# Row 0 copied and not rotated, biases of q and k as rows, zero columns left out, a sums step moved to the denominators, first sums in a fixed order

## Chip, cores, metric

One core of one Trainium2 chip. The metric is the time of one launch on the device in microseconds (us); where several runs of a kernel exist, their median. Every run quoted here is in the fast state: none took over 1.5% longer than the fastest of its kernel. TensorE is called PE in the profile, VectorE DVE, ScalarE ACT, GpSimd POOL, SyncE SP.

## The reference, cut

Two residual layers on eight images of 256 channels, 96 x 96, in f32.

```python
def gn(v, G=32, eps=1e-5): ...                 # group norm over 8 channels x H x W, no scale or shift
def layer0(x):                                 # after group norm
    q, k, v = [fft2(pconv(x, w, b)) for w, b in ((w1, b1), (w2, b2), (w3, b3))]   # 1x1 convolutions
    # 8 heads of 32 channels; q and k normalised over all positions
    attn = einsum("bhcn,bhdn->bhcd", q, k) * temperature       # complex
    attn = complex(softmax(real(attn)), softmax(imag(attn)))
    return pconv(abs(ifft2(einsum("bhcd,bhdn->bhcn", attn, v))), w_out)
def layer1(x):                                 # after group norm; linear attention, d = 32
    q, k = softplus(Wq x + bq), softplus(Wk x + bk)
    v = Wv x + bv
    norm = 1 / einsum("bnd,bd->bn", q, sum_n(k) + 1e-6)
    return einsum("bnd,bde,bn->ben", q, einsum("bdn,ben->bde", k, v), norm)
x = x + layer0(gn(x))
x = x + layer1(gn(x))                          # x: (8, 256, 96, 96) f32
```

The kernel does not compute an FFT. It takes even and odd parts of each image (a pixel and its mirror), their products over channels ("sums") for layer 0's attention, a "rotation" of each image row, and builds from these the absolute value of layer 0. Layer 1 follows image by image.

## The kernel before

Work of two images is woven on TensorE: a stage is a generator, and at each `yield` a step of another generator is put into TensorE's stream. While image b goes through its stages, the steps of the sums of image b+1 fill the gaps. A stage that yields more takes steps that would otherwise stand at the end of the output stage. (The name `own` is a scratch tile of layer 1, `xr` a transposed row, `y` a rotated row, `eo` the even and odd parts.)

```python
# the sums of one image: a generator; each yield ends one "sums step" = 4 transposes + 8 product passes on TensorE
def pair_sums(b):
    ...
    ahead = [even_odd(b, us.pop(0))]           # sums and differences of a row and its mirror, VectorE or GpSimd
    for u in range(NT - 1, -2, -1):            # u = 0: the rows that are loaded last
        ...
        for i in range(0, cols, P):
            ...
            nc.tensor.transpose(pt[...], eo[:, c, k, i:i + np_], ident)          # eoT
            ...
            products(*pending, first, False)                                    # acc
            if b and u < NT and i:
                stats_chunk(st0, b, 2 * (NT - 1 - u) + i // P - 1)
            yield
    if not b:
        for c in range(NC):
            stats_chunk(st0, b, c)

# in the attention stage: the biases of q and k are added by matmuls against the identity
for c in range(2):
    for m in range(KC):
        nc.tensor.matmul(pb[32 * m:32 * m + 1, c * P:(c + 1) * P], lhsT=b12col[:, KC * c + m:KC * c + m + 1],
                         rhs=ident, start=False, stop=(c == 1), skip_group_check=True)
yield 1
...
# in the rotation of two image rows: transpose, then multiply by the rotation of that row
for r in range(2):
    for k in range(KC):
        if h is not None:
            o = x_col(h + r)
            nc.tensor.transpose(pt[0:W, ...], x_of(b)[:, k, o:o + W], ident)     # xr
        if turned is not None:
            nc.tensor.matmul(pu[:, o:o + W + 1], lhsT=gt[0:W, r, ...], rhs=tm[:, g % TR + r, :], ...)   # y
...
# end of layer 1: denominators, attention map
nc.vector.reciprocal(rec, pd[:, 0:CH])
...
yield 1                                        # one sums step of the next image is put here
# output stage
for s in range(NS):                            # NS = 6 groups of 4 chunks
    for m in range(KC):
        ...                                    # output matmuls, additions to x
        yield 1
    if b + 1 < B and s in (1, NS - 1):
        load_x(b + 1, NT // 4 - 2 - s // 2 // 2)          # the last rows of the next image
    ...                                        # four output transfers of 384 KB

def weave(stage, other):                       # other's steps are put in where the stage yields
    due = 0
    for n in stage:
        due += n
        while due >= 1:
            next(other, None)
            due -= 1

sums = pair_sums(0)
next(sums); tables(); finish(sums)
turns = rotate(0)
for b in range(B):
    weave(attention(b), turns); finish(turns)
    sums = pair_sums(b + 1) if b + 1 < B else iter(())
    weave(images(b), sums)
    weave(layer1(b), sums)
    weave(output(b, *l1.pop(b)), sums)
    if b + 1 < B:
        turns = rotate(b + 1)
        finish(sums)                           # what steps are left come here
```

## Time and profile before

| | before |
|---|---|
| time, median of 4 runs (range) | 2778.5 us (2775.7 to 2780.7) |
| span of the profiled run | 2776.2 us |
| TensorE busy | 2731.4 us, 98% |
| mean granted clock of TensorE | 0.992 |
| TensorE's first instruction | 9.16 us |
| first transposed row of the rotation | 76.97 us |
| period of an image | 341.3 us |

The lines are in the prediction below. For this document the trace is also cut into stages, by the start of TensorE's first instruction of each kind: first transposed row (xr), first sum over rows of the rotated image (zs), first projection of layer 1 (kq), denominators (den), next image's first xr. Such a stage has a length that repeats to 0.02 us from image to image unless TensorE waits in it, so a change of 0.1 us per image can be read from one trace, where the times of whole runs scatter by 2 to 5 us. These stage lengths are read from the timeline and subtracted; the text gives them as plain numbers. The granted clock is the share of its full clock that TensorE got.

### The profile page before, as it was taken

The numbers are of one execution on the slowest core, as the hardware profiler recorded it, in microseconds if no ns is written. First come the engines' busy times: TensorE is split into PE (matmuls) and PEld (weight loads), VectorE is DVE, ScalarE is ACT, GpSimd is POOL, SyncE is SP. The second block draws the span as 40 slices with busy tenths as digits, with TensorE's granted clock in tenths as the row PEclk, the third lists the DMA queues.
The fourth block names the chain that finished last, engine by engine and source line by source line (L and its number), as shares of the span: only waits on it lengthen the run. The fifth ranks groups of instructions, "written<-read, shape, count | busy, mean of one in ns | idle before, by whom it ended". The sixth has DMA issues, their size and how long they took to land.

```text
span 2776.2 us, 47920 instructions
## 1 busy us (share of the span) xinstructions
PE 2731.4 (98%) x18460; PEld 1982.1 (71%) x18460; DVE 1950.3 (70%) x4088; ACT 1374.4 (50%) x2114; POOL 835.8 (30%) x914
## 2 busy tenths in 40 slices
PE   8999999999999999999999999999999999999988
PEld 8965679657795677956679566885678856788556
DVE  6578765876658766587675876758766687666766
ACT  3455634556345563355634546445554455544553
POOL 5033340343403424035140350413513134131311
PEclk9999999999999999999999999999999999999997
DMA  5120151201512015120151201521015210241003
GB/s 168 36 67 12 47 183 43 66 10 49 177 43 72 6 47 181 43 69 6 53 177 45 63 6 53 181 53 52 6 53 184 56 46 7 76 164 27 1 7 137
DMA packets 197810, 192.52 MB, mean 69 GB/s; under 512 B 89360, under 2 KB 197584, under 8 KB 197584
## 3 DMA queue, kind: packets, MB, share of 16 engines
q1 hardware_dynamic: 130336, 164.34, 18.6%
q10 hardware_dynamic: 67248, 25.12, 3.6%
q8 instruction: 147, 2.41, 0.4%
q14 instruction: 79, 0.65, 0.1%
HBM read 113.85 MB, written 75.57 MB: 68 GB/s over the span
## 4 chain that ended last, share of the span: by engine, by line
PE 94%; DVE 3%; ACT 2%; issue 0%; DMA 0%; POOL 0%; POOLq 0%; ACTq 0%; DVEq 0%
PE z L615 20%; PE po L627 18%; PE acc L325 13%; PE y L549 10%; PE xr L546 6%; PE eoT L344 5%; PE xT L773 5%; PE kq L712 5%; PE o L857 4%; PE kx L749 3%; PE cw L423 1%; DVE rec L819 1%; PE kT L764 1%; DVE arena L554 1%; PE mz L510 1%; PE cw L434 1%
## 5 line engine op out<-in xcount | busy, mean ns | idle before, releaser
L615 PE MATMUL z<-arena,mz 128*128 128x384 f32 (+2 forms) x2400 | 595.0, 476 | 0.0
L627 PE MATMUL po<-e,wo 128*128 128x384 f32 x1536 | 529.7, 486 | 0.2 <-ACT e L662 0.2
L661 POOL TENSOR_TENSOR e<-e 128x768 f32<-128x768 f32 x192 | 348.5, 1816 | 553.5 <-ACT e L660 553.5
L615 PEld LDWEIGHTS z<-arena,mz 128*128 128x128 f32 (+1 forms) x2400 | 325.6, 163 | 241.4 <-issue 42.4
L549 PE MATMUL y<-tm,xT 96*128 96x97 f32 x3072 | 477.6, 261 | 1.7 <-ACT sd_a L283 0.5
L549 PEld LDWEIGHTS y<-tm,xT 96*128 96x128 f32 x3072 | 462.6, 192 | 12.9 <-ACT xT L557 5.1
L325 PE MATMUL acc<-xT 128*128 128x256 f32 (+2 forms) x2368 | 440.2, 328 | 3.5 <-ACT xT L347 3.5
L627 PEld LDWEIGHTS po<-e,wo 128*128 128x128 f32 x1536 | 289.5, 190 | 197.7 <-DVE arena L629 1.2
L656 DVE TENSOR_TENSOR e<-z,xT 128x768 f32<-128x768 f32 x384 | 366.1, 953 | 88.2 <-PE z L615 88.2
L259 DVE BATCH_NORM_STATS2 st<-arena 128x6 f32<-128x384 f32 x768 | 406.3, 552 | 14.6 <-DMA arena<-in_x_dram 4.1
L546 PE MATMUL xr<-ident,arena 128*96 128x128 f32 x1536 | 413.6, 275 | 0.0
L325 PEld LDWEIGHTS acc<-xT 128*128 128x128 f32 (+1 forms) x2368 | 380.0, 191 | 37.7 <-ACT xT L347 5.2
L557 ACT COPY xT<-xr 96x512 f32<-96x512 f32 x384 | 222.2, 583 | 287.6 <-PE xr L546 286.1
L660 ACT ACTIVATE e<-e 128x1536 f32<-128x1536 f32 x192 | 284.5, 1482 | 92.6 <-DVE e L656 91.4
L662 ACT ACTIVATE e<-e 128x768 f32<-128x768 f32 x192 | 161.9, 843 | 334.4 <-POOL e L661 333.2
L311 POOL TENSOR_TENSOR eo<-arena 128x760 f32<-128x760 f32 x136 | 247.2, 1818 | 141.9 <-issue 133.3
L629 DVE TENSOR_TENSOR arena<-arena,po 128x384 f32<-128x384 f32 x384 | 211.2, 552 | 94.8 <-PE po L627 71.8
L347 ACT ACTIVATE xT<-eoT 128x512 f32<-128x512 f32 x280 | 166.8, 598 | 189.8 <-PE eoT L344 187.9
L532 POOL COPY tm<-csn 96x6 f32<-96x6 f32 x128 | 24.7, 193 | 752.0 <-PE y L549 549.7
L546 PEld LDWEIGHTS xr<-ident,arena 128*96 128x96 f32 x1536 | 230.1, 150 | 8.9 <-issue 5.6
L554 DVE COPY arena<-y 128x384 f32<-128x384 f32 x384 | 210.3, 548 | 0.8
L553 DVE COPY ys<-y 128x4 f32<-128x4 f32 x384 | 62.5, 163 | 207.2 <-PE y L549 205.1
(200 smaller groups left out, 3073.8 us busy)
## 6 DMA issues: line engine op xcount, KB each, us to landing
arena<-in_x_dram SPq DMA_DIRECT2D x184, 384.0 KB
out_dram<-arena SPq DMA_DIRECT2D x184, 384.0 KB
tm<-rt ACTq DMA_DIRECT2D x112, 216.0 KB
tm<-rt SPq DMA_DIRECT2D x16, 216.0 KB
arena<-in_x_dram SPq DMA_DIRECT2D x8, 288.0 KB
out_dram<-arena SPq DMA_DIRECT2D x8, 288.0 KB
wl<-in_w1t_dram SPq DMA_DIRECT2D x8, 256.0 KB
wl<-in_w2t_dram SPq DMA_DIRECT2D x8, 256.0 KB
```

Source lines behind the costliest of these rows:

```text
L259: nc.vector.bn_stats(out=st[:, k, c, :], in_=x_of(b)[:, k, c * CH:(c + 1) * CH])
L311: op(d[:, :, lo:hi, 1:W], x_t[:, :, ra:ra + n, 1:W], x_t[:, :, back, W - 1:0:-1])
L325: mm = nc.tensor.matmul(acc[c][:, m * C:m * C + (KC - m) * P], lhsT=t[0:np_, c, m * P:(m + 1) * P], rhs=t[0:np_, c, m * P:C], start=(first ...
L546: nc.tensor.transpose(pt[0:W, r * C + k * P:r * C + (k + 1) * P], x_of(b)[:, k, o:o + W], ident)
L549: nc.tensor.matmul(pu[:, o:o + W + 1], lhsT=gt[0:W, r, k * P:(k + 1) * P], rhs=tm[:, g % TR + r, :], start=True, stop=True)
L554: nc.vector.tensor_copy(y[:, :, :, g:g + 2], src[:, :, W - 1::-1, :])
L557: nc.scalar.copy(xt[0:W, :, 0:C], pt[0:W, :].rearrange("p (r n) -> p r n", r=2))
L615: mm = nc.tensor.matmul(out[:, o:o + n * W], lhsT=columns(mz, k, c, j), rhs=y[:, k, h * W:(h + n) * W], start=(k == 0 and o == 0), stop=(k ...
L627: nc.tensor.matmul(po[:, 0:CH], lhsT=wo[:, k, m * P:(m + 1) * P], rhs=e[:, k, :], start=(k == 0), stop=(k == KC - 1))
L656: nc.vector.tensor_add(e[:, 2 * c:2 * c + 2, :].rearrange("p t (q h) -> p t q h", h=H), pz[:, 0:CH].rearrange("p (q h) -> p q h", h=H).uns ...
L660: nc.scalar.activation(e, e, AF.Square)
L661: nc.gpsimd.tensor_add(e[:, 0:2, :], e[:, 0:2, :], e[:, 2:4, :])
```

## The change

Its intent: fewer instructions on TensorE, which is the bound (parts 1 to 3), one wait of TensorE covered by work (part 4), and an earlier start (part 5).

1. Row 0 of each image is turned by nothing, so it is copied by GpSimd; its two transposes and two matmuls go.
2. The biases of q and k lie as rows and are added by VectorE, in place of four matmuls per image.
3. 24 zero columns of a small matrix are set by a memset and not by matmuls.
4. One more sums step stands between the denominators and the broadcast of their reciprocal; the last loads are asked for ahead of the sums step that follows the output matmuls.
5. VectorE's instructions of the first image's sums are kept in program order, ahead of the table copies.

```diff
@@ -126,7 +126,10 @@
     def ps_tile(name):
         return psum.tile([P, 512], F32, tag="ps", name=name)
 
+    loaded = set()
+
     def load_x(b, t):
+        loaded.add((b, t))
         for c in (2 * (NT - 1 - t), 2 * (NT - 1 - t) + 1):
             for h, n in chunk_rows(c):
                 nc.sync.dma_start(out=x_of(b)[:, :, x_col(h):x_col(h) + n * W], in_=x_v[b, :, :, h * W:(h + n) * W])
@@ -189,14 +192,16 @@
     wkq0 = const.tile([P, KC, 2, D], F32, name="wkq0")
     for c, v in enumerate((wkt, wqt)):
         nc.scalar.dma_start(out=wkq0[:, :, c, :], in_=v.rearrange("(k p) o -> p k o", p=P))
-    b12col = const.tile([P, 4], F32, name="b12col")
+    b12 = const.tile([P, 2, P], F32, name="b12")
     b3col = const.tile([P, KC], F32, name="b3col")
     bkq4 = const.tile([P, 2], F32, name="bkq4")
     tcol = const.tile([P, KC], F32, name="tcol")
 
     def load_small():
+        nc.gpsimd.memset(b12[0:64], 0.0)
         for c, v in enumerate((b1, b2)):
-            nc.sync.dma_start(out=b12col[:, KC * c:KC * c + KC], in_=v.rearrange("(k p) -> p k", p=P))
+            for m in range(KC):
+                nc.sync.dma_start(out=b12[32 * m:32 * m + 1, c, :], in_=v[m * P:(m + 1) * P].unsqueeze(0))
         nc.sync.dma_start(out=b3col, in_=b3.rearrange("(k p) -> p k", p=P))
         temp_f = temp.rearrange("h a b -> h (a b)")
         for h in range(C // HEAD):
@@ -290,6 +295,7 @@
 
     def even_odd(b, u):
 
+        assert (b, u % NT) in loaded
         nr = PR if u < NT else 1
         t = ring_tile(f"eo_{b}_{u}").rearrange("p (c k n) -> p c k n", c=2, k=KC)
         x_t = image(x_of(b))
@@ -350,12 +356,9 @@
                     products(*pending, first, False)
                     first = False
                 pending = (t, np_)
-                if b and u < NT and i:
+                if u < NT and i:
                     stats_chunk(st0, b, 2 * (NT - 1 - u) + i // P - 1)
                 yield
-        if not b:
-            for c in range(NC):
-                stats_chunk(st0, b, c)
         s0[b] = st0, acc, products, pending
 
     y0 = {}
@@ -388,16 +391,13 @@
             for m in range(KC):
                 nc.tensor.matmul(pb[32 * m:32 * m + 2, 0:2 * P], lhsT=dmm[:, k, :],
                                  rhs=w12[:, k, :].rearrange("p (c n) -> p c n", c=2)[:, :, m * P:(m + 1) * P],
-                                 start=(k == 0), stop=False, skip_group_check=True)
-        for c in range(2):
-            for m in range(KC):
-                nc.tensor.matmul(pb[32 * m:32 * m + 1, c * P:(c + 1) * P], lhsT=b12col[:, KC * c + m:KC * c + m + 1],
-                                 rhs=ident, start=False, stop=(c == 1), skip_group_check=True)
+                                 start=(k == 0), stop=(k == KC - 1), skip_group_check=True)
         yield 1
 
         qkm = [scr[1][32 * m:32 * m + 2, 0:6 * P].rearrange("p (i c n) -> p i c n", i=3, c=2) for m in range(KC)]
         for m in range(KC):
-            nc.scalar.copy(qkm[m][:, 0], pb[32 * m:32 * m + 2, 0:2 * P].rearrange("p (c n) -> p c n", c=2))
+            nc.vector.tensor_add(qkm[m][:, 0], b12[32 * m:32 * m + 2],
+                                 pb[32 * m:32 * m + 2, 0:2 * P].rearrange("p (c n) -> p c n", c=2))
             nc.vector.tensor_scalar_mul(qkm[m][:, 1], qkm[m][:, 0], hw2[32 * m:32 * m + 2])
             nc.vector.tensor_mul(qkm[m][:, 2], qkm[m][:, 0], qkm[m][:, 1])
         pt = ps_tile(f"covT_{b}")
@@ -504,12 +504,13 @@
 
         MZ = (NZ + 3) * NH
         mz = one.tile([P, KC, MZ], F32, tag="wbig", name=f"mz_{b}")
+        nc.gpsimd.memset(mz[:, :, NZ * NH:MZ], 0.0)
         for k in range(KC):
             pm = ps_tile(f"mz_{b}_{k}")
             for m in range(KC):
-                nc.tensor.matmul(pm[:, 0:MZ], lhsT=w3n[:, m, k * P:(k + 1) * P],
-                                 rhs=at[:, m].rearrange("p n h -> p (n h)"), start=(m == 0), stop=(m == KC - 1))
-            nc.vector.tensor_scalar_mul(mz[:, k, :], pm[:, 0:MZ], rstd[:, k:k + 1])
+                nc.tensor.matmul(pm[:, 0:NZ * NH], lhsT=w3n[:, m, k * P:(k + 1) * P],
+                                 rhs=at[:, m, 0:NZ].rearrange("p n h -> p (n h)"), start=(m == 0), stop=(m == KC - 1))
+            nc.vector.tensor_scalar_mul(mz[:, k, 0:NZ * NH], pm[:, 0:NZ * NH], rstd[:, k:k + 1])
             yield 1
 
         m0[b] = mz, nmean, beta
@@ -525,6 +526,9 @@
 
         y = image(y_of(b))
         ys = one.tile([P, KC, H + 1], F32, tag="ys", name=f"ys_{b}")
+        o = x_col(0)
+        nc.gpsimd.tensor_copy(y[:, :, :, 0], x_of(b)[:, :, o:o + W])
+        nc.gpsimd.memset(ys[:, :, 0:1], 0.0)
 
         def load_r(h):
             tm = three.tile([P, TR * (W + 1)], F32, tag="tm", name=f"tm_{b}_{h}")[0:W].rearrange("p (r w) -> p r w", r=TR)
@@ -541,20 +545,22 @@
                 pu = ps_tile(f"y_{b}_{g}")
             for r in range(2):
                 for k in range(KC):
-                    if h is not None:
+                    if h is not None and h + r:
                         o = x_col(h + r)
                         nc.tensor.transpose(pt[0:W, r * C + k * P:r * C + (k + 1) * P], x_of(b)[:, k, o:o + W], ident)
-                    if turned is not None:
+                    if turned is not None and g + r:
                         o = (r * KC + k) * (W + 1)
                         nc.tensor.matmul(pu[:, o:o + W + 1], lhsT=gt[0:W, r, k * P:(k + 1) * P], rhs=tm[:, g % TR + r, :],
                                          start=True, stop=True)
             if turned is not None:
                 src = pu[:, 0:2 * KC * (W + 1)].rearrange("p (r k w) -> p k w r", r=2, k=KC)
-                nc.vector.tensor_copy(ys[:, :, g:g + 2], src[:, :, W, :])
-                nc.vector.tensor_copy(y[:, :, :, g:g + 2], src[:, :, W - 1::-1, :])
+                r = 0 if g else 1
+                nc.vector.tensor_copy(ys[:, :, g + r:g + 2], src[:, :, W, r:2])
+                nc.vector.tensor_copy(y[:, :, :, g + r:g + 2], src[:, :, W - 1::-1, r:2])
             if h is not None:
                 xt = xt_slot()
-                nc.scalar.copy(xt[0:W, :, 0:C], pt[0:W, :].rearrange("p (r n) -> p r n", r=2))
+                r = 0 if h else 1
+                nc.scalar.copy(xt[0:W, r:2, 0:C], pt[0:W, r * C:2 * C].rearrange("p (r n) -> p r n", n=C))
                 return xt
 
         tms = [load_r(g) for g in range(0, 3 * TR, TR)]
@@ -822,7 +828,7 @@
             nc.tensor.matmul(pa[:, 0:C], lhsT=kxT[:, k, :], rhs=wvs[:, k, :], start=(k == 0), stop=(k == KC - 1))
         am = own[:, 3 * C + 4:4 * C + 4]
         nc.vector.scalar_tensor_tensor(am, in0=bvs, scalar=ksum, in1=pa[:, 0:C], op0=ALU.mult, op1=ALU.add)
-        yield 1
+        yield 2
 
         l1[b] = x, kq, rec, am
 
@@ -868,9 +874,9 @@
                     if s + 1 >= 4:
                         pds.append(select(s + 1, acc_tile(f"rec_{b}_{s + 1}")))
                     normalize(s + 1, pds[s + 1])
+                if b + 1 < B and m and s in (1, NS - 1):
+                    load_x(b + 1, NT // 4 - 2 - s // 2 // 2)
                 yield 1
-            if b + 1 < B and s in (1, NS - 1):
-                load_x(b + 1, NT // 4 - 2 - s // 2 // 2)
             for j in range(NB):
                 for h, n_ in chunk_rows(NB * s + j):
                     nc.sync.dma_start(out=out_v[b, :, :, h * W:(h + n_) * W], in_=x[:, :, x_col(h):x_col(h) + n_ * W])
@@ -889,9 +895,11 @@
             pass
 
     sums = pair_sums(0)
-    next(sums)
-    tables()
-    finish(sums)
+    with tc.manual_schedule(engines={mybir.EngineType.DVE}):
+        for _ in range(NT):
+            next(sums)
+        tables()
+        finish(sums)
     turns = rotate(0)
     for b in range(B):
         with tc.manual_schedule(engines={mybir.EngineType.PE}):
```

## The prediction

> **What bounds the kernel now.** I read the profile page first, then the waits of the matrix engine (PE), then timelines of four places. From the page:
>
> ```profile
> PE 2731.4 (98%) x18460; PEld 1982.1 (71%) x18460; DVE 1950.3 (70%) x4088; ACT 1374.4 (50%) x2114; POOL 835.8 (30%) x914
> PE 94%; DVE 3%; ACT 2%; issue 0%; DMA 0%; POOL 0%; POOLq 0%; ACTq 0%; DVEq 0%
> ```
>
> PE is busy for 98% of the span and carries 94% of the chain that ends last. Every PE instruction taken out therefore shortens the run by its place in the stream, and work moved between DVE, ACT and POOL costs nothing unless PE comes to wait for it. The waits of PE (columns: waiter, releaser, total us, times, longest) show how little waiting is left:
>
> ```profile
> PE eoT L344 <- DVE eo L311: 9.4, 2, 9.2
> PE rec L833 <- DVE rec L819: 5.2, 8, 1.6
> PE eoT L344 <- POOL eo L312: 1.3, 7, 0.2
> ```
>
> The first is the start of the kernel, the second the wait for the reciprocal of the denominators, once per image. The timeline says what the start waits for (start, duration, idle before and its releaser):
>
> ```profile
> 6.01 0.39 POOL L312 TENSOR_TENSOR eo<-arena 128x8 f32<-128x8 f32 x2 [2.50 <-DMA arena<-in_x_dram]
> 7.28 0.18 DVE L234 COPY gsel<-arena 128x16 f32<-128x16 f32 x1 [2.14 <-DMA arena<-in_gmat_dram]
> 8.08 1.80 DVE L311 TENSOR_TENSOR eo<-arena 128x760 f32<-128x760 f32 x2
> 9.16 0.66 PE L344 MATMUL eoT<-ident,eo 128*128 128x128 f32 x2 [9.16 <-DVE eo L311]
> ```
>
> The rows for the first even/odd sums are in by 6.01 (POOL uses them), but DVE stands behind copies that wait for a small table until 7.28 and starts the sums at 8.08; PE follows 1.08 us later. From then on PE runs one sums step (4 transposes, 8 product passes) each 1.75 us, without a gap, until 77 us. An image then takes 341.2 us (matching PE lines at 77 and 418).
>
> **What the Trainium skill says.** "TensorE: Matmul & The Clock Gate", section "LDWEIGHTS (loading the stationary operand)": a weight load takes its columns over 1.2 GHz, 80 ns for 96 and 107 ns for 128. The trace agrees where it matters: in the rotation one transpose (96 weight columns) and the two passes of one matmul (128 each) make 80 + 107 + 107 = 294 ns, and the pattern repeats every 307 ns. The same page, "Back-to-back issue gap": about one column per cycle at 2.4 GHz. The trace's f32 passes need two cycles per column (eight passes of 384 columns in 2.58 us, 322 ns each), and a matmul of the program is two passes. "SBUF — State Buffer", section "SBUF: two separate sides": DVE and GpSimd lock a shared port for a whole instruction, so one blocks the other when both read two SBUF operands. The trace agrees: the first long POOL sum, at 8.88, takes 2.65 us instead of 1.8 while DVE is in its own.
>
> **Part 1, row 0 not rotated.** The timeline of PE at the start of image 2's attention:
>
> ```profile
> 418.44 1.04 PE L546 MATMUL xr<-ident,arena 128*96 128x128 f32 x8
> 423.29 0.28 PE L546 MATMUL xr<-ident,arena 128*96 128x128 f32 x1
> 423.40 0.36 PE L549 MATMUL y<-tm,xT 96*128 96x97 f32 x2
> 423.69 1.03 PE L389 MATMUL qkm<-wl,dmm 128*2 128x256 f32 x8
> 424.55 0.61 PE L394 MATMUL qkm<-ident,b12col 128*1 128x128 f32 x8
> 425.09 0.31 PE L546 MATMUL xr<-ident,arena 128*96 128x128 f32 x1
> ```
>
> Eight transposes occupy 418.44 to 419.32, so one is 0.11 us; a transpose with its two y passes is 0.307, so a y is 0.20. Two transposes and two y go: 2 x 0.11 + 2 x 0.20 = 0.62 us per image, **-5.0 us** for eight. The copy instead is one POOL instruction of 192 elements per partition, by scale with POOL's 1.0 us for 384 (two operands) about half a microsecond. In the built order it stands in the prologue among the sums, and for later images behind the last sums, where POOL idles 14 us (its tm copy at 423.83). It must wait for the output transfers of the image before, as the first y write of DVE did. I count nothing for it.
>
> **Part 2, biases.** L394 goes: 424.55 to 425.09 is 0.54 us per image, **-4.3 us**. The ACT copies (0.75 us for the two) become two DVE additions of 2x256, about 0.4 us each by the neighbouring DVE products (L402, 0.40). Their result is first used by matmuls at 438.8, thirteen microseconds later: nothing.
>
> **Part 3, zero columns.** Four matmuls of two passes lose 24 columns each: 8 x 24 x 2 / 2.4 = 160 ns per image, **-1.3 us**. A pass still has 264 columns (220 ns), above its 107 ns weight load.
>
> **Part 4, a sums step at the denominators.** Before, in image 1:
>
> ```profile
> 364.62 1.13 PE L822 MATMUL am<-wvs,own 128*128 128x256 f32 x4
> 365.58 0.60 PE L344 MATMUL eoT<-ident,eo 128*128 128x128 f32 x4
> 366.02 0.82 PE L325 MATMUL acc<-xT 128*128 128x256 f32 x4
> 367.35 0.93 PE L833 MATMUL rec<-rec,sel 32*128 32x384 f32 x8 [0.52 <-DVE rec L819]
> ```
>
> One sums step more before L833 covers the 0.52 us. It exists for seven images (the eighth has no next image): total 5.2 less the 1.6 of the last, **-3.6 us**. The step is not free: it comes from the end of the output stage, where seven steps followed the last output matmuls. The fourth last of all steps needs the image's last loaded rows (eo of u=0), and the load waits for those output matmuls:
>
> ```profile
> 401.95 1.22 PE L857 MATMUL o<-arena,own 32*128 32x384 f32 x8
> 407.83 1.42 DVE L311 TENSOR_TENSOR eo<-arena 128x570 f32<-128x570 f32 x2 [1.68 <-DMA arena<-in_x_dram]
> 410.15 0.60 PE L344 MATMUL eoT<-ident,eo 128*128 128x128 f32 x4
> ```
>
> From the start of the last output group, DVE could begin after 5.88 us and finished its second sum after 7.30; PE came at 8.20. Now PE comes one step (1.75) earlier, at 6.45, and reaches the two transposes that need the second sum at 6.67. In the seven images the DVE start lies at 5.88, 6.97, 5.22, 6.11, 5.4, 5.55 and 5.34; adding about 1.5 for the second sum and its wrapped column on POOL, less 6.67 (6.95 in the last, where PE came 0.28 later): waits of 0.7, 1.8, 0.05, 0.95, 0.25, 0.4, 0, together **+4.1 us**. The move thus gives back what it takes. Moving the issue of the load ahead of the sums step does not help: its transfer still waits for the same matmuls.
>
> **Part 5, first sums in fixed order.** DVE now does the first sums before any table copy, so it starts at about 6.0 instead of 8.08: PE starts about 2.1 us earlier. One table matmul also leaves PE's start (10.61 to 11.34 before) for a place where it costs next to nothing. The next sums come from POOL: their rows are in at 8.88, then two instructions of 1.8 and two of 0.2, 12.9 at best, 13.7 as before with the port lock; PE wants them at about 13.5. I take **-2.4 us**. Later DVE has to keep up with PE: in the built order it will stand at the table matmul until PE's step 12, near 29 us, and still has about 4 us before PE needs its next sums (13.5 + 15 x 1.75 = 39.8 against about 35.5).
>
> Sum: -5.0 - 4.3 - 1.3 - 3.6 + 4.1 - 2.4 = -12.5, so 2778.4 - 12.5 = **2765.9 us**, some 0.45% faster.
>
> **Rivals.** (A) The load of the last rows is no worse than before or lands earlier: then all of part 4 counts and the sum is -16.6, 2762. For it: three of the seven landings leave almost no wait. Against it: image 2 already waits a little at this place (the 1.3 us of waits above, seven times in all), so there is no reserve. (B) The load lands later, because output and input share the engines and the moved step shifts them: 2 us per image gives +14 instead of +4.1, about 2776, no gain. For it: landings vary by 1.75 us now. Against it: the load stands in the same order behind the same transfers. (C) The fixed DVE order makes PE wait in the prologue, for example at the table matmul, by a few microseconds: 2768 to 2772. Against it: the 4 us of reserve worked out above. (D) The longer DVE chain in the attention stage, or POOL behind the row copy, stalls PE: each us per image would cost 8. The slack of 13 us and POOL's 14 us of idleness speak against it.
>
> **Range and chances.** A and the best prologue (-0.5) give about 2761; B in part, or C, gives 2772. With 3 us of scatter between the runs of before I take 2760 to 2773. Leaving 2% (55 us) either way needs something none of these holds: within 2% 0.98.
>
> **What would show it right or wrong.** PE's first transpose near 7.1 us and the first rotation near 74.6. No L394, and 0.54 us less there. PE busy falls by about 11. The wait of rec for DVE falls to the last image's, about 1.6 us. A wait of eoT, by DVE or POOL eo, of about 4 us in seven pieces appears near the end of each output stage. The period of an image falls from 341.2 to about 340.0 (-0.62 - 0.54 - 0.16 - 0.52 + 0.6 = -1.24). I am wrong if the new eoT waits are absent or several times larger, if PE's start doesn't move, or if PE waits at the denominators as before.

## The result

| | before | after |
|---|---|---|
| time, median of 4 runs (range), us | 2778.5 (2775.7 to 2780.7) | 2763.6 (2762.5 to 2765.0) |
| ratio after/before | | 0.9947, 95% interval 0.993 to 0.9964 |
| predicted | | 2766 (2760 to 2773) |

Ratios are the mean time of one kernel's fast runs over that of the other's of the same rounds, so not quite the ratio of the medians quoted. A control of five further rounds in a later call gave 2765.1 us (2762.6 to 2767.8) against 2776.2, ratio 0.996 (0.9948 to 0.9973). The record calls two kernels different from 2% on, so by its measure the time is the same; but both intervals leave out 1, so a small gain is there.

From the page of the changed kernel (busy time with share and instructions; then the shares of the chain that ended last by engine):

```profile
PE 2719.5 (99%) x18348; PEld 1972.5 (71%) x18348; DVE 1958.4 (71%) x4104; ACT 1366.5 (49%) x2098; POOL 841.5 (30%) x939
PE 94%; DVE 3%; ACT 2%; DMA 1%; issue 1%; POOL 0%; SPq 0%; POOLq 0%; DVEq 0%; ACTq 0%
```

TensorE's busy time fell by 11.9 us; it is still the bound. DMA rose from 0% to 1% of the chain. The waits of TensorE (us in all, times, longest) say why:

```profile
PE eoT L350 <- POOL eo L318: 10.4, 15, 7.3
...
PE rec L839 <- DVE rec L825: 1.6, 1, 1.6
```

The wait for the reciprocal is down from eight to the one of the last image. The wait of the transposes (eoT) for POOL's part of the even and odd sums has 15 pieces. Two are the kernel's start (7.3 and 0.2). Seven, 1.3 us in all, stand 129.6 us after the start of zs in each image in which sums run, and were there before the change. Six, 1.6 us in all, are new: they stand at the end of the output stage of three images. (The view lists only waits above 0.15 us.) The start itself, from the timeline (start, duration, what; in brackets the idle time before it and its releaser):

```profile
6.19 1.82 DVE L317 TENSOR_TENSOR eo<-arena 128x760 f32<-128x760 f32 x2 [3.54 <-DMA arena<-in_x_dram]
7.29 0.67 PE L350 MATMUL eoT<-ident,eo 128*128 128x128 f32 x2 [7.29 <-POOL eo L318]
...
30.12 0.15 DVE L246 COPY arena<-pcs 96x2 f32<-96x2 f32 x1 [2.07 <-PE pcs L244]
```

DVE goes to the sums when their rows are in, and TensorE starts at 7.29 and not at 9.16. The third line is the place where DVE stands for a table matmul; TensorE did not wait there.

The stages of the two profiled runs:

| from, to | before | after | difference in the run |
|---|---|---|---|
| start, first xr | 76.97 | 75.05 | -1.9 |
| xr, zs (attention and rotation), each of images 2 to 8 | 74.90 | 73.69 | 8 x -1.21 = -9.6 |
| zs, kq, all eight | 1161.6 | 1161.5 | -0.1 |
| kq, den, images 1 to 7 | 65.06 to 65.08 | 65.05 to 65.08 | -0.1 |
| kq, den, last image | 57.78 | 55.27 | -2.5 |
| den, next xr, sum of seven | 387.22 | 385.61 | -1.6 |
| last den, TensorE's end | 30.04 | 30.08 | 0.0 |

Together -15.8 us between these two traces (-15.5 between the spans, as the last transfers end 7.6 us after TensorE before and 7.9 after). Two lines need explaining: 2.5 us in the last image, where the change did nothing, and den to xr, where a wait of 0.52 us went from each of seven images and yet the sum fell by only 1.6. In that stage TensorE has at the denominators

```profile
363.93 1.47 PE L331 MATMUL acc<-xT 128*128 128x256 f32 x8
365.33 0.93 PE L839 MATMUL rec<-rec,sel 32*128 32x384 f32 x8
```

without a wait before the broadcast (0.52 in the lines of before). And at the end of the output stage, first the queue of SP (which asks for the transfers), then VectorE, then TensorE:

```profile
399.48 2.69 SPq L135 DMA_DIRECT2D arena<-in_x_dram  x3
402.26 4.24 SPq L882 DMA_DIRECT2D out_dram<-arena  x5
```

```profile
404.49 0.62 DVE L317 TENSOR_TENSOR eo<-arena 128x190 f32<-128x190 f32 x2 [1.86 <-DMA arena<-in_x_dram]
405.79 1.42 DVE L317 TENSOR_TENSOR eo<-arena 128x570 f32<-128x570 f32 x2 [0.67 <-DMA arena<-in_x_dram]
```

```profile
406.69 0.42 PE L350 MATMUL eoT<-ident,eo 128*128 128x128 f32 x2 [0.16 <-POOL eo L318]
407.36 0.42 PE L350 MATMUL eoT<-ident,eo 128*128 128x128 f32 x2 [0.26 <-POOL eo L318]
```

Follow the chain upwards: TensorE waits for POOL's small part of eo (L318), which comes with VectorE's (L317), which waits for the rows of the last load (asked for from 399.48). This is the wait that the prediction set against the covered one. The brackets show 0.16 + 0.26 = 0.42 us of idle time, but that stage (the first of the seven) takes 55.47 us where one without a wait takes 54.65: the wait costs 0.82. The starts of the timeline tell it: these transposes begin 1.64 us after the products ahead of them, the ones before began 1.31 after theirs, and the second pair starts 0.67 after the first, where without a wait it starts 0.22 after. In two later images the wait cost 0.9 and 1.1 us (0.50 and 0.71 shown), in one 0.2, in three nothing. So the cost is no multiple of the idle time shown: where both pairs show a wait, it is 0.4 us more.

### The profile page after: what moved, and what is told of

Its sections match the earlier page's. It is cut to its first block, busy times and chain, and to the rows that moved or that the text cites. A ratio compares the mean times of both kernels' runs of the same rounds, so it can differ in the third digit from the quotient of the medians.

```text
span 2760.7 us, 47785 instructions
## 1 busy us (share of the span) xinstructions
PE 2719.5 (99%) x18348; PEld 1972.5 (71%) x18348; DVE 1958.4 (71%) x4104; ACT 1366.5 (49%) x2098; POOL 841.5 (30%) x939
## 4 chain that ended last, share of the span: by engine, by line
PE 94%; DVE 3%; ACT 2%; DMA 1%; issue 1%; POOL 0%; SPq 0%; POOLq 0%; DVEq 0%; ACTq 0%
PE z L621 21%; PE po L633 18%; PE acc L331 13%; PE y L553 10%; PE xr L550 6%; PE eoT L350 5%; PE xT L779 5%; PE kq L718 5%; PE o L863 4%; PE kx L755 3%; DMA arena<-in_x_dram 1%; PE cw L423 1%; PE kT L770 1%; DVE arena L559 1%; PE mz L511 1%
## 5 line engine op out<-in xcount | busy, mean ns | idle before, releaser
L553 PEld LDWEIGHTS y<-tm,xT 96*128 96x128 f32 x3040 | 457.8, 192 | 12.5 <-issue 4.9
L563 ACT COPY xT<-xr 96x512 f32<-96x512 f32 (+1 forms) x384 | 220.2, 578 | 293.8 <-PE xr L550 289.4
L317 POOL TENSOR_TENSOR eo<-arena 128x760 f32<-128x760 f32 x136 | 246.1, 1809 | 253.7 <-issue 130.1
L559 DVE COPY arena<-y 128x384 f32<-128x384 f32 (+1 forms) x384 | 209.7, 547 | 1.2 <-issue 0.5
L558 DVE COPY ys<-y 128x4 f32<-128x4 f32 (+1 forms) x384 | 62.4, 162 | 199.3 <-PE y L553 195.9
L350 PE MATMUL eoT<-ident,eo 128*128 128x128 f32 (+1 forms) x1184 | 188.1, 280 | 10.4 <-POOL eo L318 10.4
```

What stands on the lines that cost most here:

```text
L317: op(d[:, :, lo:hi, 1:W], x_t[:, :, ra:ra + n, 1:W], x_t[:, :, back, W - 1:0:-1])
L350: nc.tensor.transpose(pt[0:np_, c * C + k * P:c * C + (k + 1) * P], eo[:, c, k, i:i + np_], ident)
L553: nc.tensor.matmul(pu[:, o:o + W + 1], lhsT=gt[0:W, r, k * P:(k + 1) * P], rhs=tm[:, g % TR + r, :], start=True, stop=True)
L559: nc.vector.tensor_copy(y[:, :, :, g + r:g + 2], src[:, :, W - 1::-1, r:2])
```

## The experiments

All twelve gave correct results. Three calls, each with its own runs of the kernel before on the same chip: (1) no_step, late_load, q5_own, free_order; (2) row0_turned, bias_matmuls, zero_columns, warm; (3) after_again, early_load, early_warm, step_from_kq. All diffs are against the changed kernel.

| run | median us (range) | ratio to before (95%) | xr to zs, images 2 to 8 | den to xr, sum of seven | kq to den, last image |
|---|---|---|---|---|---|
| no_step | 2765.1 (2762.8 to 2766.0) | 0.9956 (0.9942 to 0.9971) | 73.69 | 386.86 | 57.57 |
| late_load | 2783.1 (2782.5 to 2785.0) | 1.0023 (1.0014 to 1.0033) | 73.69 | 404.85 | 56.84 |
| q5_own | 2766.2 (2763.0 to 2767.2) | 0.9960 (0.9946 to 0.9974) | 73.69 | 386.21 | 57.84 |
| free_order | 2767.3 (2766.5 to 2768.5) | 0.9966 (0.9953 to 0.9979) | 73.69 | 385.08 | 56.95 |
| row0_turned | 2770.2 (2768.5 to 2771.1) | 0.9973 (0.9963 to 0.9984) | 74.31 | 386.25 | 56.81 |
| bias_matmuls | 2770.6 (2767.6 to 2775.6) | 0.9975 (0.9966 to 0.9984) | 74.12 | 387.62 | 57.01 |
| zero_columns | 2765.7 (2764.2 to 2767.2) | 0.9957 (0.9942 to 0.9971) | 73.85 | 388.16 | 55.34 |
| warm | 2762.5 (2761.7 to 2765.0) | 0.9947 (0.9934 to 0.9961) | 73.69 | 388.44 | 52.81 |
| after_again | 2765.1 (2762.6 to 2767.8) | 0.9960 (0.9948 to 0.9973) | 73.69 | 387.35 | 57.77 |
| early_load | 2759.8 (2759.6 to 2761.6) | 0.9943 (0.9930 to 0.9955) | 73.69 | 382.60 | 55.33 |
| early_warm | 2759.2 (2757.3 to 2759.9) | 0.9938 (0.9925 to 0.9952) | 73.69 | 382.57 | 54.36 |
| step_from_kq | 2774.9 (2772.6 to 2776.2) | 0.9993 (0.9984 to 1.0001) | 73.69 | 395.33 | 54.97 |

### Parts 1, 2 and 3, each undone

**row0_turned**: the rotation of before, with row 0 in it.

```diff
-        nc.gpsimd.tensor_copy(y[:, :, :, 0], x_of(b)[:, :, o:o + W])
-                    if h is not None and h + r:
+                    if h is not None:
-                    if turned is not None and g + r:
+                    if turned is not None:
```

> The changed kernel with row 0 rotated again (part 1 undone). My theory: 2 transposes of 0.11 and 2 matmuls of 0.20 us come back: the stage from the first rotation transpose to the zs matmuls goes from 73.94 or less to 0.62 us more in each of the eight images, and nothing else changes; 5.0 us slower. Rival (POOL's copy, or the wait for the output transfers in front of it, gave part of the gain back): more than 0.62 per image is lost or less, and the stage denominators to rotation changes as well.

**bias_matmuls**: the biases by matmuls again, the ACT copies in place of the VectorE additions.

```diff
+        for c in range(2):
+            for m in range(KC):
+                nc.tensor.matmul(pb[32 * m:32 * m + 1, c * P:(c + 1) * P], lhsT=b12col[...], rhs=ident, ...)
-            nc.vector.tensor_add(qkm[m][:, 0], b12[32 * m:32 * m + 2], pb[...])
+            nc.scalar.copy(qkm[m][:, 0], pb[...])
```

> The changed kernel with the four bias matmuls and the ACT copies again (part 2 undone). Predicted 0.54 us per image; the stages of the changed kernel sum to 0.10 less than predicted, and if that lies here, the stage from first rotation transpose to zs grows by 0.43 us per image (8 passes of 128 columns, two at a time, are 0.427 us by the two cycles per column), 3.4 us in all. Rival: 0.54 per image and the missing 0.10 elsewhere.

**zero_columns**: the matmuls over all columns again, no memset.

```diff
-        nc.gpsimd.memset(mz[:, :, NZ * NH:MZ], 0.0)
-                nc.tensor.matmul(pm[:, 0:NZ * NH], ..., rhs=at[:, m, 0:NZ]...)
+                nc.tensor.matmul(pm[:, 0:MZ], ..., rhs=at[:, m]...)
```

> The changed kernel with the 24 zero columns in the mz matmuls again (part 3 undone). 0.16 us per image more in the stage from first rotation transpose to zs, 1.3 us in all; if the columns are hidden behind weight loads instead, nothing.

Measured: the stage from xr to zs takes 74.31, 74.12 and 73.85 us in place of 73.69: 0.62, 0.43 and 0.16 us for an image. They add up to 1.21, the whole of what the stage lost. Over eight images that is 5.0, 3.4 and 1.3 us. Parts 1 and 3 have the size that was worked out; part 2 was taken for 0.54. The timeline of TensorE with the bias matmuls shows where the 0.11 went,

```profile
420.36 1.03 PE L390 MATMUL qkm<-wl,dmm 128*2 128x256 f32 x8
421.22 0.61 PE L395 MATMUL qkm<-ident,b12col 128*1 128x128 f32 x8
421.76 0.31 PE L551 MATMUL xr<-ident,arena 128*96 128x128 f32 x1
```

and the same place of the changed kernel:

```profile
420.11 1.03 PE L392 MATMUL qkm<-wl,dmm 128*2 128x256 f32 x8
421.08 0.32 PE L550 MATMUL xr<-ident,arena 128*96 128x128 f32 x1
```

With them the next transpose starts 1.40 us after the first qkm matmul, without them 0.97. The prediction counted from the start of the bias matmuls to the next transpose (0.54 here too); but without them that transpose does not take their place at 0.86, it comes 0.11 later, because the tail of the qkm group has to be paid in either case. What a group costs is the difference of two timelines, not the distance of two starts in one.

### Part 4, undone

**no_step**

```diff
         nc.vector.scalar_tensor_tensor(am, in0=bvs, scalar=ksum, in1=pa[:, 0:C], op0=ALU.mult, op1=ALU.add)
-        yield 2
+        yield 1
```

> The changed kernel with one sums step at the denominators again (part 4 undone). My theory: the stage from the denominators to the next image's first rotation transpose goes back from 54.65 to 55.76 us (changed kernel) to 55.25 to 55.5 in each of the seven images; the wait of rec for the reciprocal is 0.52 us in each again (5.2 us in all), the split waits of eoT for the last rows go away or stay under 0.2 us each; about 1.6 us slower than the changed kernel in all, 2765 us. Rival: the step gains nothing at the denominators and its waits are chance; then the stages stay at a mean of 55.1 and the time doesn't change.

The waits of TensorE are those of before again:

```profile
PE eoT L350 <- POOL eo L318: 8.6, 9, 7.2
PE rec L839 <- DVE rec L825: 5.2, 8, 1.6
```

Each of the seven stages den to xr takes 55.26 or 55.27 us, 386.86 in sum. With the step, a stage without a wait takes 54.65 (so the seven would come to 382.6): covering the reciprocal's wait saves 0.61, a little more than the 0.52 that the wait itself shows. But the seven sums of the kernels that have the step and the same loads (the changed one, its control, free_order, row0_turned, bias_matmuls, zero_columns, warm) are 385.1 to 388.4, mean 386.9, because the transposes wait for the last rows. Gain 4.3, given back 4.3. (The other half of part 4, the load asked for ahead of the sums step, moved nothing by itself: SP asked for the half of the load that waits for the last output matmuls 40.1 us after the denominators in the kernel before and in no_step.) Over no_step three of the seven show a gain (free_order 1.8, the changed kernel 1.25, row0_turned 0.6) and four a loss of up to 1.6; the times agree, 2765.1 without the step against 2763.6 and 2765.1 with it.

### What the new wait waits for

**late_load**: the two halves of the last load in reverse order, so that the half that could go early, whose first row the first sum needs, goes after the half that waits for the last output matmuls.

```diff
-        for c in (2 * (NT - 1 - t), 2 * (NT - 1 - t) + 1):
+        for c in (2 * (NT - 1 - t), 2 * (NT - 1 - t) + 1)[::-1 if b and t == 0 else 1]:
```

> The changed kernel with the two halves of the last load of a next image in reverse order, so that the half that could go early goes after the half that waits for the last output matmuls. My theory (PE waits for the landing of these rows): the landing comes about 1 us later, the waits of eoT grow in every image, by 0.5 to 1.5 us each, 4 to 10 us in all; attention stages and start unchanged. Rival (the waits come from the POOL and DVE sums being slow, not from the transfer): no change, within 1 us.

```profile
PE eoT L350 <- POOL eo L318: 24.7, 23, 7.1
```

VectorE's first sum at this place moved from 404.49 to 407.09 and the wait before the transposes grew to 2.0 us:

```profile
408.52 0.42 PE L350 MATMUL eoT<-ident,eo 128*128 128x128 f32 x2 [2.00 <-POOL eo L318]
409.19 0.41 PE L350 MATMUL eoT<-ident,eo 128*128 128x128 f32 x2 [0.26 <-POOL eo L318]
```

den to xr grew to 404.85 in sum, and the kernel became slower than the one before. So TensorE does wait for the landing of this transfer, and each us of it costs one: in the first image the idle time shown grew from 0.42 to 2.26 us, and the stage by as much, from 55.47 to 57.31. In size the expectation missed: 18 us over the mean of the kernels with the usual order, where it said 4 to 10. The first half was asked for 3.0 us later than in the changed kernel and stood behind the other half. (In two of the seven images the wait, 2.72 and 1.93 us, was followed by 3.4 us of half clock, which made 59.7 and 58.9 of the usual 57.2; in the other five, after 1.90 to 2.00 us, it was not.)

**q5_own**: the sixth block of q lies in free columns of another tile and no longer in rows that the last load overwrites, so the load does not wait for the last output matmuls.

```diff
         def kq(c, s):
+            if c == 1 and s == NS - 1:
+                return own[:, 6 * C - CH:6 * C]
             ...
-        zero = own[:, 5 * C:5 * C + 1]
+        zero = own[:, 4 * C + 64:4 * C + 65]
```

> The changed kernel with the last normalized q block kept in free columns of another tile, so that the last load of the next image no longer waits for the last output matmuls. My theory: the load goes about 1 us or more earlier, all waits of eoT near the end of the output stage vanish, each of the seven stages from denominators to rotation falls to 54.65 or a little less; 2.6 us faster than the changed kernel, about 2761 us. Rival (waits due to transfers sharing the engines with the output): some waits stay, less than 1 us gained.

The waits stayed: 386.21 in sum, and the total of the eoT waits was 10.4 us as in the changed kernel. SP's line in this run:

```profile
399.19 2.28 SPq L135 DMA_DIRECT2D arena<-in_x_dram  x3
```

Counted from the denominators, as a mean of the seven images, SP asked for the first half when it did before (39.2 us after them) and for the second 1.1 us earlier (40.2 and not 41.3). The rows came no earlier: VectorE's first sum started at 44.8 and not 44.5. The theory that the matmuls hold up the load, which the prediction shares ("its transfer still waits for the same matmuls"), was therefore not the whole: just ahead of the load stand the four output transfers of 384 KB of s = 4, 1.6 MB. From the table of stretches of the changed kernel (stretch, length, busy time and instructions of each engine, granted clock, share of the DMA engines' time, GB/s):

```profile
400.00:402.00 2.00, 2.00 (x18) 1.28 (x17) 1.50 (x4) 0.66 (x2) 0.17 (x2) 1.00 1.03 322
402.00:404.00 2.00, 2.00 (x16) 1.89 (x15) 0.64 (x2) 0.85 (x2) 0.89 (x1) 1.00 0.99 299
404.00:406.00 2.00, 2.00 (x16) 1.87 (x15) 0.83 (x3) 0.76 (x2) 0.81 (x3) 1.00 1.06 371
```

The engines are full all the while. The load is 0.79 MB, some 2 us at 370 GB/s, and yet VectorE got its last rows 6.3 us after the first was asked for. The Trainium skill, "DMA: Bandwidth & Descriptors", section "Issuing engines are not separate DMA queues", has it that all transfers end up on the same 16 engines and interleave, whichever engine starts them; the sharing agrees.

The trace's records of single DMA packets, which its views only sum up, tell more. Packets of 1152 bytes, three image rows, are at this place those of the load's second half. The first of them moved 43.1 us after the denominators in the changed kernel, asked for at 41.3, and 43.2 in q5_own, asked for at 40.2: what was asked for earlier only stood longer. In no_step, asked for at 40.1 but with the output ahead of it asked for 1.7 us earlier, it moved at 41.4. So it is the output ahead of the load that sets its landing here, not the matmuls.

**early_load**: q5_own, and the last load is asked for after the output matmuls of s = 4, ahead of the four output transfers of that step.

```diff
-                if b + 1 < B and m and s in (1, NS - 1):
+                if b + 1 < B and m and s in (1, NS - 2):
                     load_x(b + 1, NT // 4 - 2 - s // 2 // 2)
```

> The sixth block of q goes into free columns, and the last loaded rows (t = 0) are asked for after the output matmuls of s = 4, ahead of the four output transfers of that step. Theory (the input transfer stands behind the 1.6 MB of output issued just before it on the same engines): the rows land before the sums want them, the waits of the transposes for eo vanish, all seven stages from the denominators to the next rotation take 54.65 us (sum 382.6 instead of a mean of 386.9), and the kernel is about 4 us faster than the changed one of the same rounds, near 2759.5. Rival (only the order of matmul and load, or the sums on VectorE and GpSimd, sets the wait): the waits stay, the sum stays at 385 to 388, and the time is within 1.5 us of the changed kernel's.

```profile
396.31 1.41 SPq L135 DMA_DIRECT2D arena<-in_x_dram  x3
397.83 9.47 SPq L883 DMA_DIRECT2D out_dram<-arena  x9
```

```profile
403.39 2.15 DVE L317 TENSOR_TENSOR eo<-arena 128x190 f32<-128x190 f32 x4
```

```profile
PE eoT L350 <- POOL eo L318: 8.7, 9, 7.3
```

VectorE's sums follow its earlier work without waiting, all seven stages take 54.65 to 54.66 us, and the kernel is 5.3 us faster than its control of the same rounds; the stages are 4.75 shorter. Counted from the denominators, the experiment asked for the first half 3.7 us earlier and for the second 5.4, ahead of the output; the second half's first packet moved at 38.0 us, 5.1 earlier, and its last rows were on their way by 39.3, where VectorE's sums want them at 42.5. q5_own says that 1.1 us earlier for the second half, behind the output, gave nothing. A load ahead of the output that is asked for at the old time was not run.

**step_from_kq**: one step fewer in the kq stage, so that the output stage has its seven at the end again.

```diff
-            yield 0.5
+            yield 0.5 if s >= 2 else 0
```

> The step of the sums that stands at the denominators is taken from the kq stage (one step fewer there) and not from the end of the output stage, which has its seven again. Theory (the last loaded rows are wanted one step too early in the changed kernel): the rec wait stays covered in all images but the last, the waits for eo vanish or stay under 0.2 us each, the stages from the denominators to the next rotation come to 382.6 to 383.5 us in sum, and kq's stage keeps its 65.06 us; about 3.5 us faster than the changed kernel. Rival (kq's stage needs the step because TensorE waits there for VectorE): kq's stage grows by about what is saved, and the time stays at 2763 to 2765.

This missed, in two ways. The expected sum was wrong to begin with: a step taken from kq to den lengthens den to xr by 1.75 us and should have shortened kq to den by as much. The first happened (54.65 to 56.42, so no wait of note for the rows was left there); the second did not (65.06 to 65.17), because new waits came up in kq's stage:

```profile
PE eoT L350 <- POOL eo L318: 8.8, 10, 7.1
PE xT L779 <- ACT arena L771: 8.4, 7, 1.2
PE xT L779 <- DVE xT L784: 5.0, 7, 0.7
```

13.4 us of waits in seven images, at the transposes of x, which need buffers that ACT and DVE empty. The rival's reason was right: that stage needs its sums step. Its time was not (2763 to 2765): the kernel is 9.8 us slower than the control; the stages say 8.7.

### Part 5, undone

**free_order**: the order of VectorE's first sums left to the scheduler again.

```diff
-    with tc.manual_schedule(engines={mybir.EngineType.DVE}):
-        for _ in range(NT):
-            next(sums)
-        tables()
-        finish(sums)
+    next(sums)
+    tables()
+    finish(sums)
```

(and the first image's statistics at the end of its sums, as before)

> The changed kernel with DVE's order in the first sums left to the scheduler again, tables after the first step and the statistics at the end (part 5 undone). My theory: PE's first transpose goes back from 7.29 to 9.1 us and the first rotation from 75.05 to about 77.0; everything later keeps its length, so about 1.9 us slower than the changed kernel. Rival: the scheduler reorders other stages too, and later stages differ by more than 0.3 us.

TensorE starts at 9.23 us again and reaches the rotation at 77.99, a us later than expected:

```profile
9.23 0.66 PE L350 MATMUL eoT<-ident,eo 128*128 128x128 f32 x2 [9.23 <-DVE eo L317]
```

The twelve kernels and repeats with the fixed order reach it at 74.7 to 76.1, mean 75.3; the two without at 76.97 and 77.99, 2.2 us later. That scatter is the clock's. By the traces' record of it, full clock is first granted 4.2 to 7.0 us after TensorE's first instruction, in free_order last of all, and the way from that instruction to the rotation grows with it: 67.6 us at 4.2, 67.8 at 4.7 (the changed kernel), 68.6 at 6.5 (its control), 68.8 at 7.0 (free_order). At the same clock the way is the same to 0.2 us with and without the fixed order, so part 5 is worth its earlier start: 7.2 us (mean of twelve) against 9.2 (both without), some 2.0 us.

### The last image, and the scatter between runs

The 2.5 us that the last image's layer 1 lost has no cause in the diff. In that image no sums are left to fill the gaps, and TensorE waits once 2.7 us for statistics (gm_b) and once 3.6 us before kT. After such a wait the granted clock is 0.5 for a while. The stretches of 3.4 us around the first one in the kernel before (columns as above),

```profile
2681.40:2684.80 3.40, 3.40 (x37) 1.41 (x39) 0.16 (x1) 0.00 (x0) 0.00 (x0) 0.50 0.04 7
2684.80:2688.20 3.40, 3.40 (x36) 1.57 (x32) 1.24 (x2) 2.44 (x4) 0.00 (x0) 0.70 0.00 0
```

and in the changed one:

```profile
2667.90:2671.30 3.40, 3.40 (x40) 1.57 (x42) 0.16 (x1) 0.00 (x0) 0.00 (x0) 0.55 0.02 5
2671.30:2674.70 3.40, 3.40 (x48) 1.52 (x41) 1.95 (x4) 2.62 (x4) 0.00 (x0) 1.00 0.00 0
```

By the trace's record of the clock, half clock lasts 6.8 us after each of the two waits before, and 3.4 after each in the changed kernel. The Trainium skill, "TensorE: Matmul & The Clock Gate", section "What's actually happening", says that the clock is halved after an idle window and restored after a busy one, and that the window of 3413 ns runs freely, so where it falls is chance. The trace agrees as to the lengths, 3.4 or 6.8 us. It doesn't as to the idle window: the wait here took 2.7 us and one in late_load 1.93, with TensorE busy for 1.3 of the 3.4 us before half clock began; so a window need not be idle throughout. The control shows that it is chance and not the change: the same program took 57.77 there, as the kernel before did, against 55.27 in its first profile. Of the twelve profiles without added matmuls, eight have 6.8 us of half clock after both waits (stage 56.8 to 57.8 us; the kernel before and the control are among them), two 6.8 and 3.4 (55.3), and two 3.4 after both (55.0, and 55.3 in the changed kernel's first profile).

**warm**: in the last image, twelve matmuls whose results are not read, in those two gaps.

```diff
+        if b + 1 == B:
+            for j in range(4):
+                pw = ps_tile(f"warm0_{j}")
+                nc.tensor.matmul(pw[:, 0:CH], lhsT=wo[:, 1, 0:P], rhs=pending[-1][1][:, 1, :], start=True, stop=True)
         st1s[b] = st1
 ...
+        if b + 1 == B:
+            for j in range(8):
+                pw = ps_tile(f"warm1_{j}")
+                nc.tensor.matmul(pw[:, 0:C], lhsT=nmb[:, 1, :], rhs=wvs[:, 1, :], start=True, stop=True)
```

> The changed kernel with 4 and 8 matmuls that nobody reads placed in the last image ahead of the wait for its statistics (2.7 us) and of the wait for softplus (3.6 us). Theory: the half-clock windows after these waits (in the profile before two of 6.8 us, in the profile after two of 3.4 us) are why the last image's layer 1 took 2.5 us less in the profile after and why runs scatter by 2 to 5 us; with the gaps filled, the granted clock stays full there, the stage from kq to the denominators of the last image takes 53.5 us or less instead of 55.3 (after) and 57.8 (before), and the run is 2 to 4 us faster than the changed kernel. Rival (the 2.5 us came from the change itself): no change or slower by what the added matmuls overrun.

The granted clock stayed at 1.00 and the stage took 52.81 us, 4.96 less than the control's:

```profile
2671.20:2674.60 3.40, 3.27 (x66) 1.67 (x70) 1.44 (x5) 0.23 (x1) 0.00 (x0) 1.00 0.02 5
2674.60:2678.00 3.40, 3.40 (x49) 1.44 (x41) 2.29 (x5) 3.37 (x6) 0.00 (x0) 1.00 0.00 0
```

So the clock is what the stage's length depends on. In the time of the kernel the gain doesn't show: the ratio to before is 0.9947, where the changed kernel has 0.9947 and 0.9960. This call has no run of the changed kernel, and this profile happens to have the longest den to xr of those with the same loads.

**after_again**: the changed kernel as it is, as the control of the third call.

> The changed kernel again, as it is, as a control on this chip. If the scatter between profiles is only that of transfer landings and of the clock's windows, its time is 2763.5 +- 1.5 us, the seven stages from the denominators to the next rotation lie between 54.6 and 56 us each with a sum of 385 to 388.5 us, and the last image's way from kq to its denominators takes between 55 and 58 us.

As expected, but at the edges: the median is 0.1 us above the range, and the longest of the seven stages takes 56.05 us.

**early_warm**: early_load and warm together.

> The early load and the dummy matmuls that keep TensorE busy in the last image's layer 1, together. If the two are independent: the seven stages at 54.65 us each, the last image's way from kq to its denominators 52.8 us with no half-clock window in it, time 2755 to 2758 us, the fastest of all. If the early load gave nothing, its time is that of the dummy matmuls alone, about 2762.5.

The rows landed early again (382.57), but the second half was partly missed: 54.36 us in the last image's layer 1 and not 52.8, as one stretch at half clock was left.

```profile
2664.40:2667.80 3.40, 3.40 (x49) 1.49 (x53) 0.65 (x3) 0.00 (x0) 0.00 (x0) 0.52 0.02 5
2667.80:2671.20 3.40, 3.40 (x48) 1.62 (x44) 1.53 (x3) 2.19 (x3) 0.00 (x0) 1.00 0.00 0
```

In these two profiles the twelve matmuls left none and one of the half-clock stretches; they don't rule them out. The median is 2759.2, above the expected 2755 to 2758 and 0.5 us from early_load's, and the ranges of the two overlap (2757.3 to 2759.9, 2759.6 to 2761.6). It is the fastest of all by median, 5.9 us below its control, nearly all of it from the load.

## Why the prediction was right

It held: 2763.6 and, in the control, 2765.1 us, for 2766 predicted. By its own steps:

| step | predicted, us | measured, us | from |
|---|---|---|---|
| part 1, row 0 | -5.0 | -5.0 | row0_turned, 0.62 per image |
| part 2, biases | -4.3 | -3.4 | bias_matmuls, 0.43 per image |
| part 3, zero columns | -1.3 | -1.3 | zero_columns, 0.16 per image |
| part 4, wait covered | -3.6 | -4.3 | no_step, 0.61 x 7 |
| part 4, wait for the last rows | +4.1 | +4.3 (2.5 to 5.9) | seven profiles with the step, and early_load |
| part 5, earlier start | -2.4 | -2.0 | TensorE's start in twelve profiles against two |
| sum | -12.5 | -11.7 | differences of medians: -14.9, control -11.1 |

- **The mechanism of every part was right**, but for what holds up the last load (below); what was off most is the size of two terms, and they nearly cancel, which is luck. Part 2 was too large by 0.9 us, because the tail of the group before it was counted as saved. Part 4's gain was too small by 0.7, because a wait costs more than its idle time shows.
- **The give-back was the step that mattered.** It was worked out from the landing of one transfer against the time at which TensorE arrives, for each image, and its sum came out within the scatter. Image by image it did not repeat: 0.7, 1.8, 0.05, 0.95, 0.25, 0.4 and 0 us were predicted, 0.8, 0, 0.9, 0, 0, 1.1 and 0.2 measured in the first profile, 0.3, 0, 1.4, 0.7, 1.1, 1.2 and 0.2 in the control. So that the mean is 4.3, and no nearer to 2.5 or 5.9, is in part luck. The sign "about 4 us in seven pieces" was not met as a view: 1.6 us in six pieces are shown, as a wait costs more than it shows. Against rival A the prediction also misread a line: the seven waits of 1.3 us do not stand at this place but 129.6 us after zs; at the last rows only two of the seven images waited before, 0.16 and 0.28 us by their stages. That there was no reserve held all the same. Rival A (no give-back) is refuted: none of the seven profiles comes near 382.6, the sum without it. Rival B (landings 2 us later) is what late_load makes on purpose (2.6 us); it did not occur of itself, though B's reason, that output and input share the engines, is the one that the experiments support for why the rows come late at all.
- **The reason for the late landing was put too narrowly.** "Moving the issue of the load ahead of the sums step does not help: its transfer still waits for the same matmuls" fits the change as made in its result, but only the second half of the load waited for those matmuls; q5_own removed them from its way and nothing came of it. What set the landing was the 1.6 MB of output ahead of it: the second half's first packet moved at 43.1 or 43.2 us whether it was asked for at 41.3 or 40.2.
- **Rivals C and D** did not occur: DVE did stand 2.07 us at the table matmul near 30 us, and TensorE did not wait. GpSimd's row copy and VectorE's additions cost nothing: parts 1 to 3 add up to all that their stage lost, 1.21 us.
- The period of an image fell from 341.29 to 339.84 us (first xr of image 1 to that of image 8, over seven): -1.45 where -1.24 was said; the rest is mostly that the wait for rows in that profile cost 0.43 and not 0.6 an image.
- **What the prediction did not hold** is the clock in the last image: 2.5 of the 15.5 us between the two profiled spans are chance, and 1.3 more because the first profile's waits for rows lie under the mean. How much such luck is in the medians of -14.9 and -11.1 is not known.

Left open: whether a load asked for ahead of the output, but no earlier than before, lands in time; and whether twelve matmuls, or more, would pay reliably at the last image.

## What to carry to other kernels

When work is moved to cover a wait, look up what the work needs that now runs earlier in its place: here its input was the last to land, and covering 0.6 us per image brought up 0.6 us of waiting for a transfer. The cure was to ask for the input earlier, ahead of the outputs in the queue, which needed a few free columns, and it was worth more than the move itself. And cut a trace into stages that repeat: one profile then shows 0.1 us, where whole times scatter by several us with the clock's windows and the landings.

## What the Trainium skill lacked or had wrong

- "TensorE: Matmul & The Clock Gate", section "Back-to-back issue gap": it counts one cycle per column and gives no figure for f32. Here a matmul of the program is two PE instructions of two cycles per column each (322 ns for 384 columns at full clock), four in all. "FP8 and Floating Point Precision", section "TensorE Precision Notes", has four passes for true FP32, which agrees, but the page on the matmul's time does not point there.
- The same page, section "What's actually happening", has the clock halved after at least one idle window of about 3.4 us. Here waits of 2.7 us, and in late_load one of 1.93, were enough. The half clock lasted 3.4 or 6.8 us, and the stage with two such waits took 57.8, 55.3 or, with no half clock, 52.8 us. That is as large as the changes measured here.
- "DMA: Bandwidth & Descriptors", section "Issuing engines are not separate DMA queues", says that transfers of different issuing engines interleave. Output and load are asked for by one engine here, and the load did not get in between: half of it moved first at 43.1 or 43.2 us, asked for at 41.3 or 40.2. The page has elsewhere that the descriptors of a queue start in order, but not the price: a load of 0.79 MB right behind 1.6 MB of output had its last rows used 6.3 us after the first was asked for.
- No page has a figure for what a wait of TensorE costs against the idle time that a profile shows: 0.52 us at the denominators cost 0.61, and in two pieces among the transposes 0.42 us cost 0.82, 2.26 cost 2.65.
